# An edge-gated graph layer: the edge sums two steps behind the gates, one at a time and then in pairs

## The chip, the cores and the metric

The kernel runs on one core of a Trainium2 chip. The metric is device time in microseconds of one launch, as the median of several runs. Beside it stands one profiled execution, whose trace gives every instruction of every engine. The engines are TensorE (PE, with its weight loads PEld), VectorE (DVE), ScalarE (ACT), GpSimd (POOL) and SyncE (SP, which here only issues DMAs).

## The reference

```python
pre_u = jnp.einsum('bud,dk->buk', h_t, W1[:d])
pre_v = jnp.einsum('bvd,dk->bvk', h_t, W1[d:])
hidden = jax.nn.relu(pre_u[:, :, None, :] + pre_v[:, None, :, :] + b1)
S = jax.nn.sigmoid(jnp.einsum('buvk,ko->buvo', hidden, W2)[..., 0] + b2[0])
a_t = jnp.einsum('buv,bud->bvd', S * A_a, h_t)
m_t = jnp.einsum('uv,bud->bvd', A_m, h_t) * h_t
z_t = beta1 * h_t + beta2 * (jnp.einsum('bvd,de->bve', a_t, Wa) + ba) + beta3 * (jnp.einsum('bvd,de->bve', m_t, Wm) + bm)
```

`h_t` is x, 16 graphs of 1024 nodes with 256 features in float32. `A_a` and `A_m` are one adjacency matrix of 1024 x 1024, in which about 9 entries of a column are not zero. So the gate S is needed only on edges, and both sums over u are sums over the edges that end in v.

## The kernel before

**Blocks, tiles, steps.** The 16 graphs go in 4 groups of GB = 4; the nodes v in 8 stretches of 128. A block is one group and one stretch: 32 blocks. In a block, two windows of 64 nodes v have 5 tiles each of 128 edge places, so a block has T = 10 steps and the main loop (L745) has 320. Step n handles tile n: the same 128 edges for four graphs. In each window, the 64 nodes lie in four quarters, and tile j of the window serves quarters `[[0], [0, 1], [1, 2], [2, 3], [3]][j]`.

**What a step does.**
- `fetch` (L494): an indirect DMA of GpSimd gathers, for 128 edges, a row of 8 KB from a table in HBM: pre_u of four graphs (4 KB), then h of four graphs (4 KB). It lands in one of NF = 6 places `fetched`. The place of tile n is `n % NF`.
- `expand` (L564): TensorE copies pre_v of the edge's end node to the edge's row, with a 0/1 matrix `mark` as weights, into PSUM (`pc`, 2 buffers of 2 banks).
- `gate` (L598): VectorE adds both halves into a tile `t` of its own (one buffer, L601), then for each of four graphs does relu, the product with W2 and the sum (L606, with an accumulator read). ScalarE takes the sigmoid (L609) and multiplies four times (L612) to make the gated half of the weights `left`. The other half, the adjacency value in the one-hot column of the end node, was written for all four graphs by `left_adj` (L579).
- `aggregate` (L614): TensorE sums over edges, with `left` as weights of 32 columns for a graph (16 of the plain and 16 of the gated sum) and the h half of `fetched` as the moving side. The four graphs lie side by side in the array's columns. Each float32 product is two instructions, so a tile has 8 or 16.

**What a block does beside.** `half_end` (L628) copies finished sums from PSUM on ScalarE. `turn_over` (L633) transposes them on TensorE, ScalarE copies them to `LT` (L644), and VectorE multiplies the plain half by h (`times_h`, L654). `block_end` (L659) multiplies by Wa and Wm on TensorE, ScalarE copies the result to `z` (L675), VectorE adds beta1 times h from `h_blk` (L676), and SP stores z. `halves` (L452) makes pre_v of the next block on TensorE, ScalarE and VectorE (L463); `rows` (L434) makes pre_u of a later block and stores it in the table. All of these take their PSUM from the pool `misc`, with 2 buffers of one bank. `lists` (L239) builds the edge lists; those of four of the eight stretches run between the steps 0 to about 103, in small pieces on VectorE.

**Order.** The order is written by hand (`manual_schedule`, L471): each engine executes what is emitted for it, in that order. In step n the loop emits: `aggregate(n-1)`, the fetch of tile n+5 into the place just read, `half_end`; `gate(n)`, `left_adj(n+1)`, the next `mark`; what is due in step n (`do(n)`, filled by `after(step, f)`); `expand(n+2)`; the load of `h_blk`; and then the products of `turn_over`, `block_end`, `halves` and `rows` with ScalarE's copies of them, at fixed places s = n mod 10 of a block. So TensorE's sums of tile n-1 come first in step n, and ScalarE's copies of step n come after the sigmoid of step n and before that of step n+1.

## Time and profile before

| | |
|---|---|
| median of 3 runs | 1175.09 us |
| all three | 1177.88, 1175.09, 1167.8 us |
| span of the profiled execution | 1165.8 us |
| steps 0 to 54 (start of the step's sum on VectorE) | 71.62 to 292.12 us |
| steps 55 to 109 | 292.12 to 480.83 us |
| steps 110 to 239 | 480.83 to about 897 us |
| steps 240 to 319 | about 897 to 1148 us |
| granted TensorE clock, mean | 0.976 |

The span runs from the first to the last instruction of the profiled execution; that execution's time outside the span isn't given by the page, and the shortest of the three runs is 2.0 us above the span, the median 9.3 us. Before step 0 the first edge lists and table rows are made. The rows of the table are finished in step 233, so after that TensorE has less to do per block.

In the page, engine rows give busy time, share of the span and number of instructions. A busy TensorE row includes time in which a matmul is in flight; the pace is read from the start of one group of matmuls to the start of the next. The row of stretches gives for each stretch its length, then the busy time of PE, PEld, DVE, ACT and POOL with their instruction counts, the granted clock, the share of time that the 16 DMA engines had a packet in work (it can pass 1[...]), and GB/s.

### The profile page before, as it was taken

How to read it: one execution, taken by the hardware profiler on the slowest of the kernel's cores; microseconds unless marked ns; L12 is line 12 of the kernel's file. 1: busy time of each engine (PE TensorE's matmuls, PEld its weight loads, DVE VectorE, ACT ScalarE, POOL GpSimd, SP SyncE). 2: the span in 40 equal slices, each digit the busy share in tenths (PEclk: the TensorE clock that was granted, in tenths of full speed). 3: DMA queues.
4: the chain of work that ended last, by engine and by line, in shares of the span. 5: the costliest groups of instructions: out<-in, count | busy, mean ns of one | idle time of the engine just before them, and what ended most of it. 6: DMA issues, size and time to landing. Idle time of an engine off the chain costs nothing. (4 is left out here: it accounts for less than half of the span.)

```text
span 1165.8 us, 23918 instructions
## 1 busy us (share of the span) xinstructions
PE 1092.1 (94%) x7633; PEld 723.1 (62%) x7633; DVE 1056.2 (91%) x3487; ACT 893.5 (77%) x2624; POOL 439.9 (38%) x428
## 2 busy tenths in 40 slices
PE   7867899999999999999999999999999999999986
PEld 6744666666666666666666666666666666666553
DVE  7688889888999989999999999999999999999994
ACT  2346587767887878888888888888888888888873
POOL 1556645253335333443333333333333333333330
PEclk9868899999999999999999999999999999999999
DMA  9986898999999999999999999999998998999991
GB/s 286 298 307 223 277 372 312 362 320 331 342 320 323 396 379 336 358 350 402 389 374 369 355 364 356 360 364 383 371 375 324 361 322 333 334 339 328 328 346 60
DMA packets 147048, 391.40 MB, mean 336 GB/s; under 512 B 16753, under 2 KB 105329, under 8 KB 110705
## 3 DMA queue, kind: packets, MB, share of 16 engines
q0 software_dynamic: 50016, 300.50, 68.9%
q1 hardware_dynamic: 81616, 74.99, 20.0%
q10 hardware_dynamic: 15280, 14.29, 3.7%
q8 instruction: 63, 1.03, 0.3%
q14 instruction: 73, 0.59, 0.1%
HBM read 393.78 MB, written 50.33 MB: 381 GB/s over the span
## 5 line engine op out<-in xcount | busy, mean ns | idle before, releaser
L496 POOL DMA_INDIRECT fetched<-table,uidx x320 | 341.5, 1067 | 628.3 <-PE acc L623 447.2
L606 DVE SCALAR_TENSOR_TENSOR t<-t,w_b 128x256 f32<-128x256 f32 x1280 | 478.3, 421 | 19.3 <-ACT left L612 0.5
L601 DVE TENSOR_TENSOR t<-fetched,pc 128x1024 f32<-128x1024 f32 x320 | 389.3, 1217 | 41.4 <-PE pc L569 13.9
L623 PE MATMUL acc<-fetched,left 128*32 128x256 f32 x4096 | 336.2, 391 | 31.9 <-ACT left L612 26.2
L612 ACT ACTIVATE left<-left,gt 128x32 f32<-128x32 f32 (+1 forms) x1280 | 299.3, 304 | 10.4
L569 PE MATMUL pc<-X,mark 128*128 128x512 f32 x640 | 237.6, 453 | 6.2 <-ACT mark L562 5.0
L623 PEld LDWEIGHTS acc<-fetched,left 128*32 128x32 f32 x4096 | 130.6, 109 | 179.3 <-issue 52.4
L569 PEld LDWEIGHTS pc<-X,mark 128*128 128x128 f32 x640 | 97.2, 191 | 140.0 <-issue 89.3
L609 ACT ACTIVATE gt<-sc,b_b 128x4 f32<-128x4 f32 x320 | 96.2, 301 | 43.4 <-DVE t L606 40.8
L672 PE MATMUL misc<-w_m,LT 128*128 128x256 f32 x496 | 117.2, 379 | 0.0
L672 PE MATMUL misc<-w_a,LT 128*128 128x256 f32 x496 | 117.1, 379 | 0.0
L579 ACT ACTIVATE left<-onehot,val 128x128 f32<-128x128 bf16 (+1 forms) x320 | 116.5, 364 | 0.0
L427 PE MATMUL misc<-w_v,hT 128*128 128x256 f32 x448 | 107.3, 383 | 0.0
L427 PE MATMUL misc<-w_u,hT 128*128 128x256 f32 x416 | 101.2, 390 | 5.7 <-ACT few L329 3.6
L606 DVE DVE_READ_ACCUMULATOR t<-t,w_b 128x1 f32 x1280 | 104.0, 81 | 0.0
L672 PEld LDWEIGHTS misc<-w_a,LT 128*128 128x128 f32 x496 | 93.9, 189 | 15.1
L672 PEld LDWEIGHTS misc<-w_m,LT 128*128 128x128 f32 x496 | 93.8, 189 | 14.9
L382 POOL DMA_INDIRECT val<-in_adjT_dram,vidx x80 | 85.7, 1071 | 35.1 <-issue 22.4
L427 PEld LDWEIGHTS misc<-w_v,hT 128*128 128x128 f32 x448 | 86.0, 192 | 13.9
L427 PEld LDWEIGHTS misc<-w_u,hT 128*128 128x128 f32 x416 | 79.5, 195 | 17.3 <-ACT few L329 3.7
L631 ACT COPY ev<-acc 128x512 f32<-128x512 f32 x128 | 75.5, 590 | 14.6 <-PE acc L623 4.2
L675 ACT COPY z<-misc 128x512 f32<-128x512 f32 x62 | 36.3, 586 | 58.1 <-PE misc L672 38.8
(164 smaller groups left out, 947.9 us busy)
## 6 DMA issues: line engine op xcount, KB each, us to landing
h_blk<-in_x_dram SPq DMA_DIRECT2D x31, 512.0 KB
out_dram<-z SPq DMA_DIRECT2D x31, 512.0 KB
hT<-in_xT_dram SPq DMA_DIRECT2D x28, 512.0 KB
table<-in_x_dram ACTq DMA_DIRECT2D x24, 512.0 KB
table<-tab SPq DMA_DIRECT2D x24, 512.0 KB
fetched<-table,uidx POOLq DMA_INDIRECT x320
table<-in_x_dram SPq DMA_DIRECT2D x8, 512.0 KB
table<-fetched SPq DMA_DIRECT2D x8, 512.0 KB
```

Source lines behind the costliest of these rows:

```text
L382: nc.gpsimd.indirect_dma_start(out=val[:, i, j:j + 1], out_offset=None, in_=adj_flat, in_offset=bass.IndirectOffsetOnAxis(ap=vidx[:, i, j: ...
L427: nc.tensor.matmul(p[:, bb * D:(bb + 1) * D], hT[:, 2 * h + bb, i, :], wt[:, i, :], start=(i == 0 and not begun), stop=(i == DC - 1), skip ...
L496: nc.gpsimd.indirect_dma_start(out=fetched[n % NF], out_offset=None, in_=table[g], in_offset=bass.IndirectOffsetOnAxis(ap=uidx[:, vt * NW ...
L569: nc.tensor.matmul(pcs[n][:, c], marks[n // TW][:, j * P:(j + 1) * P], cuts[k][:, w, c], start=True, stop=True)
L579: nc.scalar.activation(lefts[n][:, :m, :, 0, :], onehot[:, i, o:o + m, :].unsqueeze(2).to_broadcast([P, m, GB, V]), AF.Copy, scale=val[:, ...
L601: nc.vector.tensor_tensor(t, fetched[n % NF][:, :GD].rearrange("p (b d) -> p b d", b=GB), pcs.pop(n).rearrange("p (b d) -> p b d", b=GB), ...
L606: nc.vector.scalar_tensor_tensor(t[:, b, :], t[:, b, :], 0.0, w2_b, ALU.max, ALU.mult, accum_out=sc[:, b:b + 1])
L609: nc.scalar.activation(gt, sc, AF.Sigmoid, bias=b2_b)
L612: nc.scalar.activation(lefts[n][:, :m, b, 1, :], lefts[n][:, :m, b, 0, :], AF.Copy, scale=gt[:, b:b + 1])
L623: nc.tensor.matmul(accs[h][b * 2 * V:(b + 1) * 2 * V, r, :], left[:, i, b].rearrange("p k v -> p (k v)"), f[:, GD + b * D:GD + (b + 1) * D ...
L631: nc.scalar.copy(evs[q], accs.pop(q))
L672: nc.tensor.matmul(pz[:, bb * D:(bb + 1) * D], LTs[k][:, c, 2 * h + bb, i, :], wt[:, c, :], start=False, stop=(i == 0 and c == DC - 1), sk ...
```

## The change

- **Sums two steps behind.** A loop `while done < min(last_in, total)` calls `gather_in`, which does `aggregate`, frees the place and refills. Up to step 109 it does tile n-2 in step n. From step 110 it does tiles n-3 and n-2 in each odd step and none in the even ones. The last three steps do tile n-1.
- **Places.** `fetched` has NF = 7 places, taken from a list `free`. From step 110 there are eight: the pool of the edge lists (`lst`, whose tiles were in other pools) is closed and its memory holds the eighth.
- **The sum in place.** `add(n)` writes the sum into the pre_u half of `fetched` and no longer into `t`. It is emitted one step ahead: `add(n+1)` stands before `gate(n)`.
- **Order.** Up to step 109 `expand(n+2)` and all products with their copies stand before the gate of step n; from step 110 behind it and behind `do(n)`. The places s of `turn_over` and `block_end` are moved; the steps of the loads and `rows` of groups 2 and 3 are moved by a few.
- **Left weights.** The plain half is written for two graphs instead of four, and each copy is shared by two neighbouring graphs: the columns of a pair lie gate, plain, gate. `LT` and the products with Wa and Wm follow that order.
- **End of a block.** The result is added into `h_blk` and stored from there; `z` is gone as a tile. Up to step 109 VectorE reads the product in PSUM without a copy; from there ScalarE copies it to a used part of `LT`. Both follow one step after the product instead of two, and `times_h` of the second window also moves up by one. `h_blk` is loaded from the table's h half (4 KB rows) instead of x (four rows of 1 KB).

```diff
-    NF = 6
+    NF = 7
+    at_slot, free = {}, list(range(NF))
...
     def fetch(n):
         k, g, vt, w, j = where(n)
+        at_slot[n] = free.pop(0)
         nc.gpsimd.indirect_dma_start(
-            out=fetched[n % NF], out_offset=None, in_=table[g],
+            out=fetched[at_slot[n]], out_offset=None, in_=table[g],
...
-        lefts[n] = wk.tile([P, 2, GB, 2, V], FP, name="left")
-        nc.scalar.activation(lefts[n][:, :m, :, 0, :], onehot[:, i, o:o + m, :].unsqueeze(2).to_broadcast([P, m, GB, V]),
+        lefts[n] = wk.tile([P, 2, 2 * GB - 1, V], FP, name="left", bufs=5)
+        nc.scalar.activation(lefts[n][:, :m, 1::GB, :],
+                             onehot[:, i, o:o + m, :].unsqueeze(2).to_broadcast([P, m, GB // 2, V]),
                              AF.Copy, scale=val[:, i, j:j + 1])
...
+    def add(n):
+        t = fetched[at_slot[n]][:, :GD]
+        nc.vector.tensor_tensor(t, t, pcs.pop(n), ALU.add)
+
     def gate(n):
-        k, g, vt, w, j = where(n)
-        t = one.tile([P, GB, D], FP, name="t")
-        nc.vector.tensor_tensor(t, fetched[n % NF][:, :GD].rearrange("p (b d) -> p b d", b=GB),
-                                pcs.pop(n).rearrange("p (b d) -> p b d", b=GB), ALU.add)
+        m = len(QUARTERS[n % TW])
+        t = fetched[at_slot[n]][:, :GD].rearrange("p (b d) -> p b d", b=GB)
...
-            nc.scalar.activation(lefts[n][:, :m, b, 1, :], lefts[n][:, :m, b, 0, :], AF.Copy, scale=gt[:, b:b + 1])
+            nc.scalar.activation(lefts[n][:, :m, 2 * b, :], lefts[n][:, :m, 1 + b // 2 * GB, :],
+                                 AF.Copy, scale=gt[:, b:b + 1])
...
-        after(step + (1 if k == BS - 1 else 2), times_h)
+        after(step + (1 if k == BS - 1 or w else 2), times_h)
...
-            nc.scalar.copy(z[:, sl], pz.rearrange("p (b d) -> p b d", b=2))
-            after(step + 2, lambda sl=sl: nc.vector.scalar_tensor_tensor(z[:, sl], hb[:, sl], be1, z[:, sl],
-                                                                         ALU.mult, ALU.add))
-        after(step + 3, lambda: nc.sync.dma_start(
-            out[g * GB:(g + 1) * GB, vt * P:(vt + 1) * P, :].rearrange("b p d -> p b d"), z))
+            z = pz.rearrange("p (b d) -> p b d", b=2)
+            if step >= ROOM:
+                z = LTs[k][:, 2 * h].rearrange("p k c n -> p (k c n)").rearrange("p (b d) -> p b d", b=2)
+                nc.scalar.copy(z, pz.rearrange("p (b d) -> p b d", b=2))
+            after(step + 1, lambda sl=sl, z=z: nc.vector.scalar_tensor_tensor(hb[:, sl], hb[:, sl], be1, z,
+                                                                              ALU.mult, ALU.add))
+        after(step + 2, lambda: nc.sync.dma_start(
+            out[g * GB:(g + 1) * GB, vt * P:(vt + 1) * P, :].rearrange("b p d -> p b d"), hb))
...
+    ROOM, MORE, PAIRS = 110, 1, 110
+    ahead = NF
+    add(0)
+
+    def refill():
+        nonlocal ahead
+        while free and ahead < total:
+            fetch(ahead)
+            ahead += 1
+
+    def gather_in(n):
+        aggregate(n)
+        free.append(at_slot.pop(n))
+        fetch_val(2)
+        refill()
+        if (n + 1) % TW in (0, MID + 1):
+            half_end(n, 0 if (n + 1) % TW else 1)
+
+    done = 0
+    for n in range(total + 2):
+        k, s = divmod(n, T)
+        if n < total - 3:
+            last_in = n - 1 if n % 2 or n < PAIRS else done
+        else:
+            last_in = n
+        while done < min(last_in, total):
+            gather_in(done)
+            done += 1
+        if n % TW == 1 and n // TW + 1 < total // TW:
+            load_mark(n // TW + 1)
+        if n < ROOM:
+            if n + 2 < total:
+                expand(n + 2)
+            products(n, k, s)
+        if n + 1 < total:
+            add(n + 1)
+        if n < total:
+            gate(n)
+            if n + 1 < total:
+                left_adj(n + 1)
+        do(n)
+        if n >= ROOM and n + 2 < total:
+            expand(n + 2)
...
-            nc.sync.dma_start(hbs[k - 1], x_rows[vt * P:(vt + 1) * P, g * GB:(g + 1) * GB, :])
+            nc.sync.dma_start(hbs[k - 1].rearrange("p b d -> p (b d)"), table[g][vt * P:(vt + 1) * P, GD:])
...
+        if n >= ROOM:
+            products(n, k, s)
+        if n == ROOM:
+            assert not running and all(next(x, None) is None for x in made)
+            lists_done()
+            more = main.enter_context(tc.tile_pool(name="more", bufs=1))
+            for i in range(MORE):
+                free.append(len(fetched))
+                fetched.append(more.tile([P, 2 * GD], FP, name=f"fetched{len(fetched)}"))
+            refill()
```

## The prediction

> **What bounds the kernel now.** First I read the engines' rows of the page, then the row of stretches for four stages: steps 0 to 54, 55 to 109, 110 to 239, 240 to the end.

> ```profile
> PE 1092.1 (94%) x7633; PEld 723.1 (62%) x7633; DVE 1056.2 (91%) x3487; ACT 893.5 (77%) x2624; POOL 439.9 (38%) x428
> ```

> ```profile
> 71.62:292.12 220.50, 199.96 (x1297) 132.96 (x1296) 188.70 (x642) 153.57 (x450) 111.59 (x107) 0.94 0.89 311
> 292.12:480.83 188.71, 183.11 (x1315) 120.76 (x1314) 180.23 (x616) 154.56 (x454) 70.37 (x66) 1.00 0.95 349
> 480.83:896.90 416.07, 412.59 (x2975) 272.37 (x2974) 393.31 (x1239) 350.15 (x1043) 151.40 (x140) 1.00 0.99 367
> 896.90:1150.00 253.10, 242.10 (x1757) 152.59 (x1757) 241.10 (x763) 208.33 (x637) 80.15 (x77) 1.00 0.89 324
> ```

> No stage has one clear bound: TensorE, VectorE and the DMA engines all stand near their limit, and they wait for each other. Only stage 1 has much open idle time (VectorE 220.50 - 188.70 = 31.8 us). Next I read how VectorE spends a step in stage 4, in the order of time.

> ```profile
> 1028.97 1.22 DVE L601 TENSOR_TENSOR t<-fetched,pc 128x1024 f32<-128x1024 f32 x1
> 1030.30 0.42 DVE L606 SCALAR_TENSOR_TENSOR t<-t,w_b 128x256 f32<-128x256 f32 x1
> ...
> 1031.69 0.08 DVE L606 DVE_READ_ACCUMULATOR t<-t,w_b 128x1 f32 x1
> 1031.86 1.22 DVE L601 TENSOR_TENSOR t<-fetched,pc 128x1024 f32<-128x1024 f32 x1
> ...
> 1034.58 0.68 DVE L654 TENSOR_TENSOR LT<-LT,hT 128x512 f32<-128x512 f32 x1
> 1035.18 1.21 DVE L601 TENSOR_TENSOR t<-fetched,pc 128x1024 f32<-128x1024 f32 x1
> 1036.42 0.42 DVE L606 SCALAR_TENSOR_TENSOR t<-t,w_b 128x256 f32<-128x256 f32 x1
> ...
> 1037.82 1.22 DVE L463 TENSOR_TENSOR low<-low,X 128x1024 f32<-128x1024 f32 x1
> 1038.95 1.21 DVE L601 TENSOR_TENSOR t<-fetched,pc 128x1024 f32<-128x1024 f32 x1
> ```

> There is no wait here, yet the step is 2.89 us (1028.97 to 1031.86) where its parts would fit in less. L463 is a sum of the same size, and the next instruction starts 1.13 us after it. L601 is followed by its reader only after 1.33 us (1.24 behind another instruction), and it starts 0.09 us after the last accumulator read, where an instruction that needs nothing from it starts with it. The four products take 0.347 us each. [...] Blocks of stage 4 take 31.28 us this way, with VectorE full.

> Last, TensorE's pace in groups, and the waits.

> ```profile
> 1037.47 1.07 PE L623 MATMUL acc<-fetched,left 128*32 128x256 f32 x16
> 1038.47 0.73 PE L569 MATMUL pc<-X,mark 128*128 128x512 f32 x2
> ...
> 1040.86 0.64 PE L623 MATMUL acc<-fetched,left 128*32 128x256 f32 x8
> 1041.43 0.73 PE L569 MATMUL pc<-X,mark 128*128 128x512 f32 x2
> ```

> ```profile
> PEld acc L623 <- ACT left L612: 50.7, 87, 3.9
> ACT X L461 <- PE misc L427: 45.7, 50, 3.3
> ACT gt L609 <- DVE t L606: 40.8, 52, 2.5
> ACT z L675 <- PE misc L672: 38.8, 48, 1.8
> ```

> Sixteen column products take 1.00 us, eight 0.57: 8 x 0.054 and a fixed 0.137 us. The four waits form a ring: TensorE's sums wait for `left`, its products stand behind the sums, ScalarE's copies wait for the products, and the next sigmoid stands behind the copies.

> [...] L601 starts 0.09 us before L463 ends, and a reader of its result 0.11 after. [...] sixteen products held up by `left` take 1.6 us and count as busy. [...]

> **The change part by part.**

> *VectorE's step.* With `add(n+1)` ahead of `gate(n)` no instruction needs the one before it: 1.13 + 4 x 0.347 = 2.52 us. Today the mean is (31.28 - 3.69)/10 = 2.76, where 3.69 us are the block's other five instructions (2 x 0.67 for z, 2 x 0.60 for LT, 1.13 for low). A block's VectorE work falls to 25.2 + 3.7 = 28.9 us. If the gap were a fixed cost of the waits, it would stay: bounds 0 and -2.4 us a block. I take the full 2.4, as the row of L463 shows the short spacing for the same size.

> *TensorE.* Its work in a block of stage 3, by starts: 10 x 0.569 for `pc`, 4 x 0.569 + 6 x 1.001 sums, 2 x 1.82 `rows`, 2 x 1.82 + 0.46 `halves`, 4 x 1.82 + 0.47 `block_end`, 1.84 transposes: 31.29 us, which is what blocks 18 and 20 took, from their first L601 to that of the next. So stage 3 is bound by TensorE and VectorE at once. [...] 5 x 0.137 = 0.69, leaving 30.6; in stage 4, without `rows`, 27.0. Sums two or more steps late no longer wait for `left`.

> *ScalarE.* Half as many plain weights: (386 - 332) ns x 192 + (332 - 310) x 128 = 13 us; no z copies in the first ten blocks: 20 x 586 ns = 12 us. Nothing waits for ScalarE alone, so I count both at zero. VectorE's reading of z from PSUM costs what it does from SBUF (0.747 us in the row of L713, 0.747 in that of L676). What it adds: each of these two `misc` buffers is held until `do(step + 1)`, so another product may wait for VectorE. Bounds 0 and 0.5 us each, 0 to 10 us; I take 3.

> *Waits that come closer.* From step 110 the copies of z and LT stand behind the sigmoid, and VectorE wants them one step after. Behind that wait stand `add` and all gates. The copy ends about 0.33 + 0.95 + 0.35 + 0.6 = 2.2 us after the gate (rows of ScalarE), VectorE comes to it after 2.5. Bounds 0 and 0.5 us, three times a block: 0 to 31 us; I take 0.15 each, 10 us in all, inside the stage sums below.

> *DMA.* The bytes stay. `h_blk` goes from 512 packets of 1 KB to 128 of 4 KB (45 and 159 ns each in the trace's packets): (512 x 45 - 128 x 159)/16 = 0.17 us of the engines a block. The store of `h_blk` must end before its next load; on SP only loads of `hT` and stores of `tab` stand behind that, due steps later: zero, with a step of lead as cover.

> *Places.* A place is now held from `add(n)` to the sum, four steps with seven places, four or five with eight. That leaves 3 to 4 steps of lead for a gather, some 9 to 12 us. Today issue to landing has a median of 8.7 us and a tenth above 10.1 (steps 120 to 159, from the trace's landing times), and VectorE waited for it 2.8 us in all. GpSimd issues two gathers back to back (0.99 us each). Zero, while TensorE keeps up.

> *Sums by stage.* Stage 1: VectorE's work is 188.7 - 55 x 0.24 = 175, the DMA engines' 0.89 x 220.5 = 196; the ring is opened. I take 203 (bounds 196 and 220): -17. Stage 2: DMA 0.95 x 188.7 = 179, VectorE 167: I take 182: -7. Stage 3: TensorE 412.6 - 13 x 0.69 = 404, DMA 0.99 x 416 = 412 at a share of 1.00 and 400 at 1.03, which 550 to 600 us shows (396 GB/s): I take 403: -13 (bounds -4 and -16). Stage 4: VectorE 80 x 2.89 = 231 and 4 of waits: -14 against 249. The start and the tail stay. Together -51 us.

> The sum is against the span of 1165.8, so 1114.8; the profiled execution lies at least as high as its span, and the median of the runs is 9.3 above it. From the median: 1175.1 - 51 = **1124**.

> **The rivals.**

> *Half of it.* The DMA engines give no more than a share of 0.99 in stage 3, or VectorE's gaps only shrink: stage 3 gives 3, stages 1 and 2 half (12), stage 4 eleven: 26 us, **1149**. For it: the share of 0.99. Against: 1.03 for 50 us, and stage 4 has room (0.89).

> *Starved, slower.* TensorE, the fullest engine of stage 3, runs a step behind VectorE. Then the first place of a pair comes free only 3 steps of 3.07 us before its `add`, 9.2 us. Two gathers are issued at once, so today's late landing of 10.1 us becomes the usual one, and each of 65 pairs waits 0.9 us: +59, and stage 3's 13 are lost: 1175 - 38 + 59 = **1196**. It decides from a landing time of 9.2 us on; today's median is 8.7. Against it: the eighth place, and lead and landing both shrink with fewer waits.

> *Nothing.* The ring closes elsewhere, through the two `misc` buffers or the copies behind the sigmoid: both upper ends above (10 + 31 us) leave 51 + 13 - 41 = 23, of which the DMA limit of the first rival, 25, leaves nothing: **1175**. That the edits don't do what they say isn't likely: the order on the engines is the emitted one.

> **How the numbers follow.** As forecast (1097 to 1140) 0.61, half 0.20, nothing 0.07, starved 0.09, better than 1097 0.03. Faster by over 1% is the forecast, the half and the better case: 0.84; same 0.07; slower 0.09. A change within 1% is about what these runs can't tell from none (they spread over 0.9%). The range reaches from both floors of stages 1 and 3 at once, 1175 - 51 - 7 - 3 with some 15 us of the spread of runs (1099), to the worse end of the half case (1164).

> **What would show it.** Right: L601 follows the accumulator read without a gap and the next product 1.13 us later; blocks of about 29 us in stage 4, 31 in stage 3; groups of 24 sums in 1.43 us; hardly any wait of sums for `left`. Wrong: VectorE waiting for `fetched`, with a DMA share under 0.95 in stage 3; waits of L676 and L654 for ScalarE; blocks that stay at 31.3 us.

## The result: 1.6% slower, and the profile after

The changed kernel takes 1191.79 us (median of four runs, 1182.81 to 1194.27) against 1171.44 us for the kernel before on the same chip: a ratio of 1.016, with an interval of 1.013 to 1.020. The profiled execution took 1194.27 us, its span is 1192.4. The forecast was 1124. Medians are over all runs of a kernel; the ratios leave out single runs that lie over 1.5% above the kernel's fastest, so the two can differ by a few tenths of a per cent. Times by stage below run from the first `add` of one stage to that of the next.

The engines' row of the page of the kernel after:

```profile
PE 1065.5 (89%) x7633; PEld 729.4 (61%) x7633; DVE 1023.6 (86%) x3487; ACT 859.9 (72%) x2604; POOL 440.5 (37%) x428
```

TensorE's products, VectorE and ScalarE are less busy than before, in absolute time too; weight loads and GpSimd stand where they were. So the change took work away and put waiting in its place. Where, the row of stretches by stage says (columns: stretch and its length, busy time of PE, PEld, DVE, ACT, POOL, granted clock, DMA share, GB/s):

```profile
71.83:295.11 223.28, 195.09 (x1273) 128.51 (x1273) 180.41 (x629) 143.40 (x433) 112.08 (x107) 0.94 0.87 306
295.11:480.40 185.29, 177.82 (x1298) 117.22 (x1297) 176.46 (x614) 144.73 (x441) 69.70 (x67) 1.00 0.98 359
480.40:919.72 439.32, 404.88 (x3014) 282.84 (x3013) 380.69 (x1246) 343.51 (x1054) 146.86 (x144) 0.98 0.95 350
919.72:1169.40 249.68, 226.81 (x1696) 152.41 (x1694) 230.39 (x760) 197.68 (x622) 84.13 (x75) 0.96 0.88 321
```

Stage 1 (steps 0 to 54) is 2.8 us longer than before, stage 2 3.4 shorter, **stage 3 (steps 110 to 239) 22.6 longer**, stage 4 0.8 shorter, the end 5 longer. (The last `add` now stands a step earlier, so the end holds a step more: in e9 below, which puts the `add` back, it takes 20.6 us, against 20.4 before and 25.7 here.) What is new is the clock: 0.98 and 0.96 in stages 3 and 4, where it was 1.00 before.

VectorE's step is what the forecast said. Its instructions in stage 4, in order of time (start, duration):

```profile
1065.62 1.22 DVE L467 TENSOR_TENSOR low<-low,X 128x1024 f32<-128x1024 f32 x1
1066.75 1.21 DVE L606 TENSOR_TENSOR fetched<-fetched,pc 128x1024 f32<-128x1024 f32 x1
1067.88 0.41 DVE L614 SCALAR_TENSOR_TENSOR fetched<-fetched,w_b 128x256 f32<-128x256 f32 x1
...
1069.27 0.08 DVE L614 DVE_READ_ACCUMULATOR fetched<-fetched,w_b 128x1 f32 x1
1069.27 1.21 DVE L606 TENSOR_TENSOR fetched<-fetched,pc 128x1024 f32<-128x1024 f32 x1
```

The `add` (now L606) starts with the accumulator read, its successor 1.13 us later, and the step is 1069.27 - 1066.75 = 2.52 us. But blocks don't take what such steps make. The waits of stages 3 and 4 (us in all, times, longest):

```profile
DVE fetched L606 <- PE pc L574: 39.0, 22, 3.7
...
PE misc L431 <- ACT LT L686: 21.8, 11, 3.7
...
DVE fetched L606 <- PE acc L631: 18.1, 10, 3.0
PE misc L435 <- ACT LT L652: 17.2, 8, 2.2
```

VectorE waits for TensorE (`expand`, L574, and what stands ahead of it). TensorE in turn waits for a ScalarE copy out of a `misc` buffer: 11 times for the copy of z (L686) and 8 times for that of LT (L652). Neither wait was there before. This is one of the eleven, in stage 3, first on TensorE and then on ScalarE:

```profile
784.88 0.60 PE L649 MATMUL misc<-ident,ev 128*128 128x128 f32 x4
787.28 1.99 PE L431 MATMUL misc<-w_u,hT 128*128 128x256 f32 x8 [1.80 <-ACT LT L686]
789.21 1.93 PE L631 MATMUL acc<-fetched,left 128*32 128x256 f32 x32
791.07 0.73 PE L574 MATMUL pc<-X,mark 128*128 128x512 f32 x2
```

```profile
785.24 0.30 ACT L617 ACTIVATE gt<-sc,b_b 128x4 f32<-128x4 f32 x1
785.57 0.96 ACT L619 ACTIVATE left<-left,gt 128x32 f32<-128x32 f32 x4
786.43 0.33 ACT L584 ACTIVATE left<-onehot,val 128x64 f32<-128x64 bf16 x1
786.67 0.56 ACT L686 COPY LT<-misc 128x512 f32<-128x512 f32 x1
```

`rows` of step 8 (L431) needs the buffer that step 7's z is in. The copy that frees it stands behind a sigmoid and its weights. TensorE comes to it at once, because step 8 is an even step and has no sums; it stands still for 1.80 us, and behind it stand a lump of 32 sums (1.86 us) and the `expand` that VectorE wants. The second place is in stage 4, and it shows something more:

```profile
1047.41 0.60 PE L649 MATMUL misc<-ident,ev 128*128 128x128 f32 x4
1050.16 0.80 PE L435 MATMUL misc<-b_p,unit 128*128 128x512 f32 x1 [2.15 <-ACT LT L652]
1050.75 3.62 PE L431 MATMUL misc<-w_v,hT 128*128 128x256 f32 x8
1054.30 2.46 PE L631 MATMUL acc<-fetched,left 128*32 128x256 f32 x24
```

```profile
1049.50:1056.30 6.80, 6.14 (x29) 3.84 (x33) 4.29 (x18) 3.59 (x11) 0.00 (x0) 0.50 0.68 263
1056.30:1063.10 6.80, 6.80 (x55) 4.67 (x48) 5.64 (x19) 5.58 (x18) 3.62 (x4) 1.00 0.76 274
```

After the wait of 2.15 us eight products take 3.62 us in place of 1.89, and 24 sums 2.46 in place of 1.50. The granted clock of that stretch is 0.50. Ten such dips, stretches at half clock, lie in stages 3 and 4, eight of 3.4 us and two of 6.8, each at a wait: 41 us at a clock of 0.50, in which, by an estimate of half of them, some 20 us of work are lost. The kernel before has none between 480 and 1150 us. Blocks of stage 3 take 32.7 us without a dip and 34.3 with one, blocks of stage 4 30.3, and 32.0 or 33.2 with a dip.

### The profile page after: what moved, and what is told of

Same layout as the page of the kernel before. It is cut to its first block, busy times and chain, and to the rows that moved or that the text cites. A ratio compares the mean times of both kernels' runs of the same rounds, so it can differ in the third digit from the quotient of the medians.

```text
span 1192.4 us, 23738 instructions
## 1 busy us (share of the span) xinstructions
PE 1065.5 (89%) x7633; PEld 729.4 (61%) x7633; DVE 1023.6 (86%) x3487; ACT 859.9 (72%) x2604; POOL 440.5 (37%) x428
## 4 chain that ended last, share of the span: by engine, by line
PE 42%; ACT 25%; DVE 20%; issue 9%; DMA 3%; another core or an unknown queue 0%; ACTq 0%; POOL 0%; DVEq 0%; POOLq 0%
PE misc L431 14%; PE acc L631 12%; DVE fetched L614 8%; ACT left L619 8%; PE pc L574 7%; DVE fetched L606 6%; PE misc L680 4%; ACT X L472 4%; ACT gt L617 2%; ACT mark L567 2%; ACT left L584 2%; PE misc L435 2%; DVE low L467 2%; ACT ev L639 2%; PE misc L649 1%
## 5 line engine op out<-in xcount | busy, mean ns | idle before, releaser
L606 DVE TENSOR_TENSOR fetched<-fetched,pc 128x1024 f32<-128x1024 f32 x320 | 388.4, 1214 | 116.5 <-PE pc L574 75.1
L614 DVE SCALAR_TENSOR_TENSOR fetched<-fetched,w_b 128x256 f32<-128x256 f32 x1280 | 474.9, 417 | 0.0
L631 PE MATMUL acc<-fetched,left 128*32 128x256 f32 x4096 | 290.4, 389 | 18.8 <-ACT left L619 8.1
L574 PE MATMUL pc<-X,mark 128*128 128x512 f32 x640 | 232.7, 452 | 13.2 <-ACT mark L567 5.0
L631 PEld LDWEIGHTS acc<-fetched,left 128*32 128x32 f32 x4096 | 123.5, 110 | 150.3 <-issue 56.7
L574 PEld LDWEIGHTS pc<-X,mark 128*128 128x128 f32 x640 | 103.0, 190 | 111.9 <-issue 63.9
L431 PE MATMUL misc<-w_u,hT 128*128 128x256 f32 x416 | 106.9, 406 | 23.8 <-ACT LT L686 18.1
L431 PE MATMUL misc<-w_v,hT 128*128 128x256 f32 x448 | 115.1, 403 | 0.0
L431 PEld LDWEIGHTS misc<-w_u,hT 128*128 128x128 f32 x416 | 82.5, 202 | 39.4 <-ACT LT L686 20.3
L584 ACT ACTIVATE left<-onehot,val 128x64 f32<-128x64 bf16 (+1 forms) x320 | 102.8, 321 | 0.0
L614 DVE DVE_READ_ACCUMULATOR fetched<-fetched,w_b 128x1 f32 x1280 | 101.2, 79 | 0.0
L431 PEld LDWEIGHTS misc<-w_v,hT 128*128 128x128 f32 x448 | 91.6, 204 | 13.9
L639 ACT COPY ev<-acc 128x512 f32<-128x512 f32 x128 | 73.6, 575 | 25.7 <-PE acc L631 19.9
L649 PE MATMUL misc<-ident,ev 128*128 128x128 f32 x512 | 79.0, 277 | 9.3 <-DVE h_blk L687 2.5
```

The source lines that it names most:

```text
L431: nc.tensor.matmul(p[:, bb * D:(bb + 1) * D], hT[:, 2 * h + bb, i, :], wt[:, i, :], start=(i == 0 and not begun), stop=(i == DC - 1), skip ...
L574: nc.tensor.matmul(pcs[n][:, c], marks[n // TW][:, j * P:(j + 1) * P], cuts[k][:, w, c], start=True, stop=True)
L584: nc.scalar.activation(lefts[n][:, :m, 1::GB, :], onehot[:, i, o:o + m, :].unsqueeze(2).to_broadcast([P, m, GB // 2, V]), AF.Copy, scale=v ...
L606: nc.vector.tensor_tensor(t, t, pcs.pop(n), ALU.add)
L614: nc.vector.scalar_tensor_tensor(t[:, b, :], t[:, b, :], 0.0, w2_b, ALU.max, ALU.mult, accum_out=sc[:, b:b + 1])
L631: nc.tensor.matmul(accs[h][b * 2 * V:(b + 1) * 2 * V, r, :], left[:, i, 2 * b - b % 2:2 * b - b % 2 + 2].rearrange("p k v -> p (k v)"), f[ ...
```

## The experiments

The theory after this reading, **Copies**: the copies behind the sigmoid hold `misc`, TensorE stands still (once a block in stage 3, once in stage 4), and the clock, which falls to 0.50 in ten dips at such waits, doubles the loss. Rivals: **Lumps** (the two tiles' sums stand ahead of `expand`, whatever the copies do), **Places** (the products were moved to bad steps), and that VectorE's shorter step was worth nothing. Several chips were used; the kernel before took 1169 to 1171 us on all but the last, so ratios to its runs on the same chip are what is compared. The kernel after stands at 1.016.

### e1_add_ahead: VectorE's part alone

The kernel before, with

```diff
+            add(n + 1)
         if n < total:
             gate(n)
```

where `add` writes into `fetched`, so that no product comes right behind the sum that it reads, as in the kernel before (the chain over `t`).

> The kernel before with one part of the change alone: the sum of step n+1 stands ahead of the four products of step n and is written in place; order, lag, places and products stay. If the forecast's price of the chain over t is right and nothing else gives way, a VectorE step of stage 4 falls from 2.89 to 2.52 us where nothing waits, stage 4 loses 10 to 14 us, stage 3 at most 4 (TensorE's 31.29 us a block stay), and the run takes 1150 to 1162 us. If VectorE only comes sooner to a wait for TensorE (expand is wanted a gate earlier, and sums one step behind still wait for left), the gap goes but the time stays: 1168 to 1178 us, with VectorE's waits for pc up by what its work lost.

1182.42 us, ratio 1.013 (1.008 to 1.019). Steps of 2.51 us appear, and the blocks of stage 4 stay at 31.3 us (247.3 us for the stage, 247.8 before). Between 896 and 1150 us VectorE now waits for `pc`, which it never did there in the kernel before; 13.1 us of this lie in stage 4:

```profile
DVE fetched L600 <- PE pc L569: 15.5, 34, 1.3
```

So the 31.28 us of a block in stage 4 were not VectorE's alone, though VectorE had no gap. A loop of the same length fits it: gate, sigmoid, `left`, sums one step behind, `expand`. Stage 3 lost 9 us, with 14.7 us of waits for gathers (`fetched`), 2.1 before; stage 1 lost 3 us more.

### e2_copies_first, e3_no_pairs, e4_old_steps: one part undone each

```diff
-        if n < ROOM:
-            if n + 2 < total:
-                expand(n + 2)
-            products(n, k, s)
+        if n + 2 < total:
+            expand(n + 2)
+        products(n, k, s)
...
-        if n >= ROOM and n + 2 < total:
-            expand(n + 2)
...
-        if n >= ROOM:
-            products(n, k, s)
```

> The changed kernel with expand and the products ahead of the gate in every step, as it has them up to step 110; all else stays, the places within a block too. Theory Copies (the copies of z and LT that stand behind the sigmoid keep both misc buffers, TensorE waits 1.8 to 2.2 us twice a block[...]): the waits of L431 and L435 for LT go from 42 us to under 10, stage 3 falls by 15 to 25 us, the run takes 1160 to 1175 us, the dips to half clock mostly vanish. Theory Lumps (sums of two tiles together stand ahead of expand): no change of more than 5 us, 1187 to 1195 us. Theory Ring (ScalarE then waits for the products ahead of its sigmoid as in the first 110 steps): slower than after, 1195 to 1210 us.

1160.32 us, ratio 0.990 (0.985 to 0.995). In the last block of this kernel two products read LT before VectorE has multiplied it with h, so the results of that block are not right, and its end, 32.8 us against 25.7 in the kernel after, says nothing; the blocks ahead of it do what the diff says. TensorE's waits for z fell from 21.8 to 4.1 us, those of L435 for LT are no longer among the larger ones, and of the ten dips two are left before the last block. From step 160 on undisturbed blocks of stage 3 take 30.6 to 30.9 us, those of stage 4 28.8: the forecast's floors.

```diff
-    ROOM, MORE, PAIRS = 110, 1, 110
+    ROOM, MORE, PAIRS = 110, 1, BS * T
```

> The changed kernel with the sums one tile at a time throughout, still two steps behind. Theory Lumps: VectorE's waits for pc at the turn of a block in stage 3 (75 us in all) fall by half in spite of 0.69 us more TensorE work a block, the run takes 1170 to 1182 us. Theory Copies: the two waits a block for LT stay at 1.8 to 2.2 us, [...] the run takes 1190 to 1206 us.

1162.73 us, ratio 0.994 (0.992 to 0.996): better than both theories said, and by its number it speaks for Lumps. Its waits point elsewhere: TensorE's waits of L431 for z are gone and those of L435 for LT fall from 17.2 to 10.6 us, though no copy was moved.

```diff
-        z = 3 if n < ROOM else 4
+        z = 3
...
-        if ROOM <= n < total - T:
-            if s in (8, 9):
-                turn_over(k, 0, s - 8, n)
-        elif s == 7 and k < BS:
+        if s == 7 and k < BS:
```

> The changed kernel with the kernel before's places for the products of a block from step 110 on (block_end in steps 3 to 6, both transposes of the first half in step 7); the order within a step stays gates first. Theory Places (the moved products fill the steps at the turn of a block): stage 3 falls by 10 to 20 us, the run takes 1172 to 1182 us. Theory Copies: the rows' product of step 8 now waits for the copies of LT behind the sigmoid of step 7 instead of that of z; a wait of 1.5 to 2.5 us a block stays, the run takes 1186 to 1200 us.

1161.74 us, ratio 0.995 (0.991 to 0.998), faster than either expected. Stage 4 takes 230.2 us in place of 247.0. Blocks of stage 3 take 32.6 us, no less than undisturbed ones of the kernel after: two waits of about 1 us a block stay in the place of one of 1.8, and what is gone is the dips, of which this trace has none in stages 3 and 4. From step 110 on:

```profile
PE misc L435 <- ACT tab L447: 11.7, 11, 1.1
PE misc L431 <- ACT LT L652: 9.0, 10, 0.9
```

Each of three quite different edits takes back 2.2 to 2.6%, more than the change had lost. That fits a loss in which no one part is slow by itself and which needs three things together: copies behind the sigmoid, a step without sums, and a product that needs the buffer in just that step. The next runs test that reading.

### e5_even_pairs and e6_z_early: the empty step

```diff
-            last_in = n - 1 if n % 2 or n < PAIRS else done
+            last_in = n - 1 if n % 2 == 0 or n < PAIRS else done
```

> The changed kernel with the pairs of sums issued in even steps in place of odd ones; all else stays. Theory Empty step (the step without sums lets TensorE go straight from the last product of step 7 to the rows' product of step 8, and in stage 4 from the transposes of step 9 to the product of halves in step 0; both want a misc buffer whose copy stands behind a sigmoid): with 1.4 to 1.9 us of sums ahead of them in even steps the waits of L431 and L435 for LT fall from 42 us to under 12, most dips to half clock go, and the run takes 1158 to 1172 us. Theory Lumps (two tiles' sums ahead of expand): nothing changes but the parity, 1185 to 1198 us.

1169.84 us, ratio 0.997 (0.995 to 1.000). There are as many pairs and as large lumps ahead of `expand`, and the loss against the kernel before is gone: Lumps falls. Undisturbed blocks of stage 3 take 30.7 us. What remains are other waits of the same kind, the transposes for the copy of `ev` (33.9 us, 30 times), with dips of their own: 37.5 us at half clock in stages 3 and 4, nearly the 41 of the kernel after. What this edit wins is therefore not won by the clock.

```diff
-        z = 3 if n < ROOM else 4
+        z = 3
```

> The changed kernel with block_end alone back in steps 3 to 6 after step 110; the transposes stay in steps 8, 9, 0 and 2. Theory Empty step: the wait of stage 3 (rows of step 8 for the copy of z of step 7) goes, stage 3 falls from 439 to about 420 us; the wait of stage 4 (halves for the copy of LT of step 9) stays, and stage 4 stays at 247 us: 1168 to 1177 us. Theory Places of the transposes: no gain from block_end alone, 1185 to 1195 us.

1166.89 us, ratio 0.999 (0.996 to 1.001). Stage 3 takes 417.3 us (expected 420) with blocks of 31.3, stage 4 242.1. Moving z alone brings stage 3 back to the 416.7 us of the kernel before; L431 waits for z no longer. L435 still waits for LT, in both stages:

```profile
PE misc L435 <- ACT LT L652: 22.2, 19, 1.3
```

In stage 4 five of these waits go with a dip, though they last only 1.3 us: blocks take 29.7 us without a dip and 31.3 with one.

### e7_filled: the clock by itself

```diff
+        if (s == 8 and ROOM <= n < 240) or (s == 0 and 240 <= n < total - T):
+            again_(n + 2)
```

where `again_` does the two products of `expand` twice more into the same `pc`: work that changes nothing. What it asks is how much of the loss the dips make, the 41 us at a clock of 0.50 in the kernel after.

> The changed kernel with four useless column products ahead of each of the two products that wait for misc (step 8 of stage 3, step 0 of stage 4): expand of two tiles on is done twice more into the same pc, 1.14 us of TensorE in a wait of 1.8 to 2.2 us. Theory Clock ([...] that, not the wait, makes most of the loss): the ten dips go and with them some 1.7 us each, 1172 to 1182 us. Theory Wait (the late copy holds TensorE whatever it does meanwhile): the wait shrinks by 1.14 us, the time stays within 4 us, or grows where the products weren't held up, 1187 to 1200 us.

1175.83 us, ratio 1.006 (1.005 to 1.008): **useless work ahead of the wait makes the kernel faster**, by 12 us if the ratios are compared, by 16 if the medians are. The granted clock over 40 slices of the page, after and then filled:

```profile
PEclk9878799999999999999999999999999989989998
```

```profile
PEclk9878899999999999999999999999999999999999
```

Two dips are left of ten, stage 3 is 9.6 us shorter, stage 4 9.7. Blocks of stage 3 take 32.6 to 32.7 us, just what blocks without a dip took before. So the clock makes 12 us (by the ratios) to 19 us (in the traces) of the loss. The wait's own part is what is left to the edits that remove it: 32.7 - 31.3 = 1.4 us a block of stage 3 to e6, 2.0 to e5.

### e8_first_old: two repairs together

The edits of e2 (but the last block gates first) and of e4.

> The changed kernel with expand and the products ahead of the gate in every step but those of the last block, and with the kernel before's steps for the products of a block (block_end 3 to 6, transposes of the first half in step 7). Both repairs at once: if they cure the same wait, no more is won than by the better of them, 1150 to 1162 us; if the copies-first order cures one wait and the old steps another, 1135 to 1150 us, with stage 3 blocks of 30.6 us and stage 4 blocks of 28.9.

1162.86 us, ratio 0.994 (0.992 to 0.996): no more than either by itself. It has the transposes' waits for `ev` instead (33.9 us, 27 times), and five dips in stage 3; why these waits come with this pair of repairs was not followed up.

### e9_chain: what VectorE's gap costs once the sums don't hold it

```diff
-        if n + 1 < total:
-            add(n + 1)
         if n < total:
+            add(n)
             gate(n)
```

on the kernel of e4.

> The kernel of e4_old_steps with the chain over t put back: the sum of step n directly ahead of its own products, sums of edges still two steps behind and in pairs. Theory Both (VectorE's chain costs 0.24 to 0.37 us a step, but shows only once the sums no longer hold the step, which is why the add ahead alone won nothing): stage 4 goes from 230 to 245 to 250 us, stage 3, held by TensorE, by at most 6, 1174 to 1186 us. Theory Lag alone (the two steps of lag won stage 4, the chain costs nothing): within 4 us of e4_old_steps, 1158 to 1166 us.

1173.52 us, ratio 1.002 (1.000 to 1.005), against 0.995. Stage 4, without and with the chain:

```profile
901.00:1131.00 230.00, 211.53 (x1704) 141.78 (x1697) 227.81 (x752) 196.85 (x620) 79.62 (x76) 1.00 0.95 353
```

```profile
899.20:1148.90 249.70, 225.21 (x1707) 152.59 (x1707) 235.60 (x751) 198.97 (x617) 75.45 (x74) 0.94 0.90 322
```

The chain costs 20 us of stage 4 here (of the whole kernel 0.8% by the ratios, some 9 us), and nothing in e1: the add ahead and the lag win something only together (stage 4: neither 247.8, add alone 247.3, lag and pairs alone 249.7, both 230.2). The clock has a share in it again. With the chain `expand` waits for VectorE to free `pc` (23.7 us, 15 times, up to 2.6) and seven dips come; the one block without a dip takes 30.3 us against 29.1, so the chain itself is worth 1.2 us a block, half the 2.4 of the forecast; about half of the 20 us is the chain's and half the clock's. By the same one block the lag without the add ahead would be worth 1 us (31.3 before), without the dips.

### e10_first_two_h and e12_first_two_h_single: a version that is faster

In e2 one block, steps 140 to 149, took 38.1 us: TensorE waited 6.6 us for hT, whose load stood on SP behind the next block's load of h_blk, and that behind the store of h_blk:

```profile
SPq L856 <- DMA out_dram<-h_blk: 26.3, 3, 15.6
```

The forecast had put this at nothing, "with a step of lead as cover".

```diff
-            hbs[k - 1] = big.tile([P, GB, D], FP, name="h_blk", bufs=1)
+            hbs[k - 1] = (more.tile([P, GB, D], FP, name="h_blk2") if n > ROOM and k % 2 else
+                          big.tile([P, GB, D], FP, name="h_blk", bufs=1))
```

on the kernel of e2, the last block gates first.

> The kernel of e2_copies_first with the last block gates first as in the changed kernel, and with a second h_blk for odd blocks after step 110, so that a block's load no longer waits for the store of the block before and the loads of hT behind it on SP start sooner. Theory Store (the store takes over 15 us, and the load of hT that stands behind the next load of h_blk comes late; this, not TensorE, makes the block of steps 140 to 149 take 38 us): that block falls to 31 us, the wait of 6.6 us for hT goes, 1142 to 1155 us. Theory Buffers (hT's own places come free late): the block stays at 38 us, 1154 to 1164 us.

1147.31 us, ratio **0.980 (0.977 to 0.984)**: faster than both kernels. Stages 3 and 4:

```profile
483.10:892.30 409.20, 397.08 (x3011) 279.97 (x3010) 377.93 (x1246) 342.90 (x1051) 154.05 (x143) 0.99 0.99 376
892.30:1118.40 226.10, 216.47 (x1688) 144.82 (x1682) 226.10 (x749) 196.15 (x617) 85.40 (x76) 1.00 0.96 356
```

Blocks take 30.8 us in stage 3, where the forecast's floor is 30.6, and 28.8 in stage 4 (floor 28.9), with VectorE busy for every microsecond of it. In undisturbed blocks of stage 3 TensorE is busy 98% of the time and the DMA share is 1.00 to 1.01 (620.7 to 836 us), so what holds the 30.8 us may be either. The block of steps 140 to 149 takes 32.2. Of the gain over e2 in the traces, 12 us lie in stage 3, 4 in stage 4 and 7 at the end, where the last block's order differs. The second `h_blk` is no full cure: in e13, which has it too, TensorE waits 8.4 us for hT in the block of steps 130 to 139.

e12 is the same kernel with sums of one tile at a time (`PAIRS` as in e3).

> The kernel of e10_first_two_h with the sums of one tile at a time. Here neither order nor places hold TensorE up, so it shows what pairs are worth by themselves. Forecast's term [...]: undisturbed blocks of stage 3 go from 30.6 to 31.3 us, stage 4 stays with VectorE at 28.9, 6 to 10 us slower than e10_first_two_h. Theory Lumps (two tiles at once make others wait): faster than e10_first_two_h by 3 us or more.

1179.61 us, ratio 1.009 (1.005 to 1.013): pairs are worth 32 us in this order, where they cost 26 in that of the kernel after (by the ratios). Blocks take 32.7 and 30.4 us. That is 1.9 and 1.6 us more than in e10, of which the forecast's term for pairs would be 0.69: its estimate from the fixed 0.137 us of a group of sums, with five groups fewer a block. The rest fits with sums that wait for `left` again, since ScalarE waits for TensorE's products ahead of its sigmoid; two groups of sums of e12 in stage 4, one held up and one not:

```profile
1061.05 1.67 PE L631 MATMUL acc<-fetched,left 128*32 128x256 f32 x16
...
1063.74 1.07 PE L631 MATMUL acc<-fetched,left 128*32 128x256 f32 x16
```

How the rest divides was not measured. Where hardly anything holds TensorE, in undisturbed blocks of stage 3 with gates first, a block takes 31.5 us with single sums (e3) and 30.7 with pairs (e5): 0.8 us, near the forecast's 0.69.

### e11_gates_first and e13_pairs_from_0: the first 110 steps

e11 is e4 with gates ahead of `expand` and products from step 0.

> The kernel of e4_old_steps with gates first, and expand and products behind them, in the first 110 steps too. Theory Order (copies first makes ScalarE's sigmoid wait for TensorE's products, and that keeps the forecast's 24 us of stages 1 and 2 away): stages 1 and 2 fall from 408 to 385 to 398 us, 1138 to 1152 us. Theory TensorE (stage 1 has eight more rows' products and the lists' own, and TensorE has no room for more): within 5 us of e4_old_steps, 1157 to 1167 us. Slower than 1170 us would say that the copies-first order is what these steps need.

1186.37 us, ratio 1.013 (1.009 to 1.016). Stages 1 and 2 go from 407.7 to 427.7 us; VectorE's waits for TensorE's `pc` in them from 29.5 to 53.2 us. Sums hardly wait for `left` any more (2.1 us of TensorE's time, 4.7 in e4), so that wait is not what holds these steps. Half clock lasts 52 us there, against 32 in e4; half of that difference, some 10 of the 20 us, can be the clock's, as an estimate. Copies first is the better order there, yet it wins nothing against the kernel before.

```diff
-    ROOM, MORE, PAIRS = 110, 1, 110
+    ROOM, MORE, PAIRS = 110, 1, 0
```

on the kernel of e10.

> The kernel of e10_first_two_h with pairs from the first step on in place of step 110. Theory Ring (with the products ahead of the gate, sigmoids wait for TensorE's products, and single sums then wait for left; pairs ask for left half as often, which is why they are worth 32 us late): the same order stands in steps 0 to 109 with single sums, so pairs there win 8 to 20 us of the 408 us of stages 1 and 2: 1128 to 1140 us. Theory DMA and lists (stage 2 has a DMA share of 0.98, stage 1 waits for its lists and their products): within 6 us of e10_first_two_h, 1141 to 1153 us.

1133.91 us on a chip on which the kernel before takes 1149.02: ratio 0.988 (0.986 to 0.990), less good than e10's 0.980 on another chip. Against e14 below, on the same chip and with the same instructions but for the pairs up to step 110, stages 1 and 2 take 401.0 us in place of 390.3. The sums' waits for `left` fall as the theory Ring said, from 7.1 to 2.6 us of TensorE's time, and yet pairs cost 11 us there. Two other things came with them. Only seven places stand before step 110, and VectorE waits for gathers (whole run; 23.9 us of it before step 110, 5.7 in e14):

```profile
DVE fetched L606 <- DMA fetched<-table,uidx: 28.8, 27, 3.0
```

And half clock lasts 45.6 us in stages 1 and 2, against 21.7 in e14, with five dips in stage 2 that e14 doesn't have. So this run doesn't say what pairs would win there with a place more.

### e14_seven_places: the eighth place

```diff
-    ROOM, MORE, PAIRS = 110, 1, 110
+    ROOM, MORE, PAIRS = 110, 0, 110
```

on the kernel of e10.

> The kernel of e10_first_two_h without the eighth place. It prices the term that the forecast counted at zero. Theory Lead (pairs hold a place for up to five steps; seven leave two to three steps of 3 us to a gather that takes 8.7): VectorE waits for fetched in every second step of stage 3, 1165 to 1200 us. Theory Zero (landing is faster than that): within 5 us of e10_first_two_h, 1142 to 1153 us.

1137.52 us, ratio 0.990 (0.989 to 0.992). Stage 4 takes 240.0 us against 226.2 in e13, stage 3 408.7 against 411.3. VectorE's waits for gathers from 480 to 1115 us:

```profile
DVE fetched L606 <- DMA fetched<-table,uidx: 32.2, 28, 4.1
```

In e13, with eight places on the same chip, they are 4.9 us. The eighth place is worth 14 us in stage 4. In stage 3 e13 loses some 9 us to the one block that waits for hT; apart from it, most of e14's blocks there are longer too (about 31.1 us against 30.8). Against e10 the whole is 1.0% by the ratios. Neither theory's number was right: the lead is short by a microsecond, not by a gather.

## Why the prediction was wrong

**The step that failed** is the paragraph on ScalarE and its copies ("Nothing waits for ScalarE alone, so I count both at zero ... each of these two `misc` buffers is held ...: I take 3"), together with "Waits that come closer". The late copies were seen, but priced for one reader only: VectorE, which wants their result. TensorE, which wants their buffer back, was given 0 to 0.5 us a buffer, and that for the buffers that VectorE reads in the first 110 steps. VectorE's part was sized well (12 us of L687's waits in stages 3 and 4 for the 10 taken). TensorE's was 39 us of waits, some 2 us each, and it lay on the path, because TensorE is the fullest engine of stage 3. Shown by e2, e5 and e6: each takes away one of the three conditions, and the wait goes (in e6 that of stage 3, the one it aims at), and with it the loss against the kernel before. Of the 78 us between the forecast's -51 and the 27 by which the profiled execution is longer, 36 lie in stage 3 and 13 in stage 4, where these waits are; 23 lie in stages 1 and 2, which they don't explain, and 5 at the end.

**The granted clock** was no term of the sum at all. It made 12 to 19 us of the loss (e7). The repairs don't win by it alike: e4 wins much of its 2.2% by it, e5 hardly any of its 1.9%. What it took, waits of TensorE of about 2 us where there had been none above 1.4, was what the paragraph above should have found.

**VectorE's step** was right to the hundredth (2.52 us). What was wrong is what it is worth: nothing alone (e1), since stage 4 had, as e1 and e9 together say, a second limit of the same length; with the lag and no waits the forecast's 28.9 us a block came out (28.8 in e10). "VectorE full" was a true reading and no proof of a bound.

**TensorE's** floor of 30.6 us a block of stage 3 came out (30.6 in e2, 30.8 in e10), though with a DMA share of 1.00 to 1.01 in those blocks it isn't shown that TensorE alone sets it. The pairs' term of 0.69 us was too small in one order (1.9 in e12) and of the wrong sign in the other (e3), where a step without sums is also a step in which TensorE runs ahead to the wait; where neither holds TensorE, it was about right (0.8, e3 against e5).

**Stages 1 and 2**: forecast -24, measured -1. The order there is the better one of two (e11); whether pairs would help is open (e13). Stage 2 stands at a DMA share of 0.98 and gave 3.4 us of the forecast's 7. For stage 1 I wrote "the ring is opened" and took -17 us. In the kernel after it was not opened there: TensorE's waits of sums for `left` and for the gates' values are 12.0 us (13.2 before), and since products now stand ahead of the gate, ScalarE's waits for TensorE rise from 42.7 to 67.0 us and VectorE's from 13.2 to 35.2. Where the sums' waits do nearly go (2.1 us in e11, 2.6 in e13), the stage is no shorter for it. What bounds it is open: TensorE is busy 195 of 223 us there, VectorE 180, and the same instructions took 223.5 us on one chip (e10) and 208.1 on another (e14).

**DMA and places.** The store of h_blk at zero was wrong where the cover was gone (up to 15.6 us of wait on SP in e2); in the kernel after no wait of TensorE for hT shows after step 110. Places at zero held, thanks to the eighth: without it, in the kernel of e10, VectorE waits 32 us for gathers (e14).

**The rivals.** *Nothing* named the mechanism, the two `misc` buffers and the copies behind the sigmoid, and gave 1175: its price lacked TensorE's side and the clock. *Starved* gave 1196, near the result by luck, by a mechanism that the trace doesn't have: in the kernel after gathers land 4 us (median, stage 3) ahead of their `add`. With seven places it does come (e13, e14). Of the signs that the forecast named, "waits of L676/L654 for ScalarE" came in a third form, as waits of TensorE for the same copies.

## What to carry to other kernels

When an order is changed so that copies out of PSUM come later, ask of every copy who waits for its buffer, not only who waits for its result, and look at what stands right ahead of that product in the matmul queue: a step that was emptied there turns a harmless lateness into a standstill (1.80 us in the block shown; in e5, where that step has sums, such waits fall from 21.8 to 5.7 us in all). An engine without a gap may share its bound with a loop of the same length; then two edits win only together, and each alone measures as nothing (stage 4: 247.8 us before, 247.3 and 249.7 with one edit, 230.2 with both). Try parts in pairs before one is thrown away: the same pairs of sums cost 2.2% in one order and won 2.9% in the other.

## What the runs showed of the hardware

The kernel before took 1149.02 us on one chip (median, with e13 and e14) and 1170.66 on another (with e12), a difference larger than what most edits here are worth.
